# A fifth float16 tile for the attention weights, the position table made in place, and the weights' squares one row tile sooner

## The chip, the cores and the metric

The kernel runs on one core of one Trainium2 chip. Five engines work side by side, each with its own instruction queue executed in order: TensorE (PE, matrix products; its weight loads are listed as PEld), VectorE (DVE), ScalarE (ACT), GpSimd (POOL) and SyncE (SP), whose queue issues all of this kernel's DMA transfers. Tiles live in SBUF, with 128 partitions; matrix products land in PSUM banks. The metric is the time of one execution on the device in microseconds. Before the change it was measured in three runs: median 1084.36 us, 1083.74 to 1086.06.

## The reference

One layer on x of 1024 rows and 512 columns. After a layer norm, xn feeds an attention and a feed-forward network, and the output is x + attention * silu(ffn).

```python
q, k, v = xn @ Wq.T, xn @ Wk.T, xn @ Wv.T      # 32 query heads, 8 key/value heads, 128 wide
q, k = rmsnorm(q, q_norm_w), rmsnorm(k, k_norm_w)
scores = q @ k.T / sqrt(128)                   # four query heads share a key head
rel = pos[None, :] - pos[:, None]
bias = where(rel > 0, -1e30, slopes[head] * rel)
attn = softmax(scores + bias) @ v
s = attn @ Wo.T                                # to 512 columns
g = silu((silu(xn @ gate) * (xn @ up)) @ down) # dequantized int weights, 1792 wide
out = x + s * g
```

The slopes are a geometric series over the 32 heads: head i has `start * start**i` with `start = 2**(-0.25)`. Four heads on, the slope is half as large.

## The kernel before

**Precision.** Most operands are split into a high and a low part of float16 (or of a 32-bit format that TensorE takes in one pass), and a product is three matmuls: high by high, high by low, low by high (`mm3`, L106 to L110).

**Stages.** The feed-forward network comes first, up to about 216 us. Then twelve projections (L981), in the order kv, q, q four times over: each `kv` makes two key and two value heads, each `q` the four query heads of one group. The attention's steps begin between the row tiles of the last two projections and go on alone after them, to the end.

**A projection** goes through eight row tiles t of 128 rows. `tile(t)` (L543) is twelve matmuls into one PSUM bank of two tags with two buffers each, a copy to SBUF on ScalarE (L553) and, on ScalarE too, sums of squares (L555); in a `kv`, ScalarE also casts the value half (L567) and VectorE subtracts (L568). Between the row tiles the next projections are prepared (`prepare`, L641). For a projection k + 2, whose weights are loaded during t = 0 to 3, `squares` (L480) runs on ScalarE ahead of row tile 7: for a `q` four squares of 128 x 512 with their accumulated sums and a small cast to `sb`; for a `kv` two of these, the cast, and one square of 128 x 1024. In the next projection, ahead of row tile 1, `norms` (L492) multiplies `sb` by ones on TensorE (L496), and VectorE makes from it the scales by which the weights are split, a head for each row tile from t = 2. Each half of a projection's rows is normalised some steps later: POOL multiplies (L609), VectorE splits into halves (L621, L622), SP transposes (L627) and stores (L632, L634).

**The attention** has 128 units, in the order of 8 groups, 4 query blocks of 256 rows and 4 heads; the blocks of a group go by `ORDER` = 2, 3, 0, 1 (the first group 3, 2, 1, 0, the last 2, 3, 1, 0), so that blocks of up to 768, 1024, 256 and 512 keys follow each other. Each unit has two query tiles, and step n (L921) puts these on the queues:

- TensorE: `scores` of tile n into one of two double banks;
- ScalarE: `heads_hi` of a unit that is done; VectorE and ScalarE: `exponentials` of tile n - 1. VectorE adds the positions `trel[g]` to the scores into a float32 tile `pf` (five buffers) and takes the minimum (L814), which frees the bank; ScalarE takes the exponential with its sum (L815);
- ScalarE: `split_hi` of tile n - 3 writes the scaled high half into a `p16` tile (L825);
- VectorE: `split_lo` of tile n - 4 writes the low half into it (L834); SP transposes the tile by DMA into `pT` (L835);
- VectorE: `heads_lo` (L868) and the sums of the output projection;
- TensorE: `values` of tile n - 9 (`AV_LAG`), which takes half of the keys for both query tiles of a unit, and matmuls of the output projection.

The order on each queue is that of the program; nothing is reordered. A `p16` tile is 4096 bytes in each partition, and there are `P16_BUFS = 4` (L62): `split_hi` of a tile waits until the transpose of the fourth tile before it has landed.

**The positions.** L732 to L734 make once, on POOL, a float32 table `nrel` of 4096 bytes in each partition, an iota with 1e20 where a key lies after the query. `relative(g)` (L787) makes from it `trel[g]`, one of two buffers, times a factor `rc` of each partition and the slope of the group's last head (L790); VectorE multiplies by the head's ratio in L814. `relative(0)` is called ahead of projection 9, with the first loads of keys, values and queries (L982 to L986), the others in the third block of the group before.

Of the kernel before, what the change touches and what calls it, by code (L numbers as in the profile page):

```python
# [10 lines left out]
F32 = mybir.dt.float32  # L11
# [5 lines left out]
ALU = mybir.AluOpType  # L17
# [4 lines left out]
P = 128  # L22
S = 1024
# [3 lines left out]
NH = 4  # L27
# [3 lines left out]
NT = S // P  # L31
# [27 lines left out]
GATE_SUMS = [27, 28, 30, 31]  # L59
GATE_STEP = 2  # L60
PF_BUFS = 5
P16_BUFS = 4  # L62

_START = 2 ** (-(2 ** (-(math.log2(H) - 3))))
SLOPES = np.array([_START * _START**i for i in range(H)], dtype=np.float32)
# [5 lines left out]
def attention_gated_by_ffn_kernel(ctx, tc, x, gu_w, gu_z, gu_s, dn_w, dn_z, dn_s, wq, wkv, wo, qnw, knw, out):  # L71
    nc = tc.nc
    ve, se, ge, te, sp = nc.vector, nc.scalar, nc.gpsimd, nc.tensor, nc.sync
# [46 lines left out]
    rc = const.tile([P, 1], F32, name="rc")  # L120
# [334 lines left out]
    def finish_step():  # L455

        for f in finishing.pop(clock[0], ()):
            f()
        clock[0] += 1
# [181 lines left out]
    def prepare(k, t):  # L641

        if k < len(projections):
            p = projections[k]
            if t == -1:
                p.squares()
            elif t == 1:
                p.norms()
            elif t == 2:
                p.scale()  # L650
            elif t == 6:
                p.factors()
            if 2 <= t < 2 + p.n:
                p.split_head(t - 2)
            elif p.kind == "kv" and 4 <= t < 6:
                p.split_values(t - 4)
# [72 lines left out]
    vp16 = left.enter_context(tc.tile_pool(name="values", bufs=1))  # L729
    fq = ctx.enter_context(tc.tile_pool(name="finish", bufs=2, side="right"))  # L730
    ap1 = ctx.enter_context(tc.tile_pool(name="attn1", bufs=2, side="right"))
    nrel = ap1.tile([P, S], F32, name="nrel", bufs=1)  # L732
    ge.iota(nrel, pattern=[[-1, S]], base=S - P, channel_multiplier=1, allow_small_or_imprecise_dtypes=True)
    ge.affine_select(nrel, nrel, pattern=[[-1, S]], compare_op=ALU.is_ge, fill=1e20, base=S - P, channel_multiplier=1)  # L734

    def queue_half(p, half):

        last = p is projections[-1]

        def due(steps, i, f):  # L740
            t = half * HT + i
            c = TILES - early + BS * (NB * (1 + t // 2) + FINISH_BLOCK) + 4 * (t % 2) if last else clock[0] + i
            finishing.setdefault(c + steps, []).append(f)

        due(0, 0, lambda: p.inverse(half))
        if p.by_root:
            due(1, 0, lambda: p.newton(half, True))
        else:
            for i in range(3):
                due((i + 1) // 2, 0, lambda i=i: p.newton(half, i == 0))  # L750
        for i in range(HT):
            t = half * HT + i
            due(4, i, lambda t=t: p.halves(t))
            due(2, i, lambda t=t: p.normalize(t))
# [5 lines left out]
    trel, pT, oT, wor = {}, {}, {}, {}  # L760

    def load_keys(g):
        kT[g] = ap1.tile([P, NT, 2, P], F16, tag="kT", name=f"kT{g}")
        sp.dma_start(kT[g].rearrange("p t a k -> p t (a k)"), kd[g // 2][:, g % 2])

    def load_values(g):
        vT[g] = ap1.tile([P, NT, 2, HD], F16, tag="vT", name=f"vT{g}")
        sp.dma_start(vT[g].rearrange("p t a d -> p t (a d)"), vd[g])

    def load_queries(g, qb):  # L770
        qT[g, qb] = ap1.tile([P, NQT, 2, NH, P], F16, tag="qT", name=f"qT{g}_{qb}")
        sp.dma_start(
            qT[g, qb].rearrange("p t a g q -> p t (a g q)"), qd[g][qb * NQT : (qb + 1) * NQT].rearrange("t p c -> p t c")
        )
# [11 lines left out]

    def relative(g):  # L787

        trel[g] = ap1.tile([P, S], F32, tag="trel", name=f"trel{g}")
        ge.tensor_scalar(trel[g], nrel, rc, float(SLOPES[g * NH + NH - 1]), ALU.mult, ALU.mult)  # L790

    s_ps, pf, rows16, p16, av_ps, op_ps = {}, {}, {}, {}, {}, {}

# [24 lines left out]
    def split_hi(u, qt):  # L818
# [4 lines left out]
        nk = pf[u, qt].shape[1]  # L823
        p16[u, qt] = ap1.tile([P, NT, 2, P], F16, tag="p16", name=f"p16_{u}_{qt}", bufs=P16_BUFS)[:, :nk]
        se.activation(p16[u, qt][:, :, 0, :], pf[u, qt], AF.Copy, scale=scale[:, qt : qt + 1])  # L825
# [95 lines left out]
    def step(n):  # L921
        nonlocal last_ps
        if n < nn:
            u, qt = order[n]
            g, qb, hh = units[u]
            b = u // NH
            if qt == 0 and hh == 1 and b + 1 < nb:
                load_queries(*blocks[b + 1])
            if qt == 0 and hh == 3 and g + 1 < HKV:
                if b % NB == KEYS_BLOCK:  # L930
                    relative(g + 1)
                    load_keys(g + 1)
                elif b % NB == VALUES_BLOCK:
                    load_values(g + 1)
            scores(u, qt)
# [41 lines left out]
                act(w, r // 2)  # L977

    last_ps = None
    early = 0  # L980
    for k, p in enumerate(projections):  # L981
        if k == len(projections) - 3:  # L982
            load_keys(0)
            load_values(0)
            load_queries(*blocks[0])
            relative(0)  # L986
        for t in range(NT):
            prepare(k + 1, t)
            if t == NT - 1:
                prepare(k + 2, -1)  # L990
            if k + 2 < len(projections) and t < KT:
                projections[k + 2].load(t)
            if t == HT:
                p.undo()
            p.tile(t)
            finish_step()
            if t % HT == HT - 1:
                queue_half(p, t // HT)
            if k >= len(projections) - 2 and t % 2 == 0:
                step(early)  # L1000
                early += 1
# [46 lines left out]
```

## Time and profile before

| | |
|---|---|
| median of three runs | 1084.36 us |
| the profiled execution | 1086.72 us |
| its span, first to last instruction | 1084.9 us |
| TensorE busy | 1023.0 us, 94% |
| VectorE busy | 879.7 us, 81% |
| ScalarE busy | 796.2 us, 73% |
| POOL busy | 351.5 us, 32% |
| ScalarE's waits at L825 for a transpose to land | 73.6 us, 56 times |
| TensorE's waits at L108 for a transpose to land | 24.4 us, 18 times |
| mean granted TensorE clock | 0.99 |

The profile is one execution; its times are microseconds from the first instruction. A group of instructions is shown as line, engine, operation, tile written and tiles read, forms and count, then the busy time, the mean duration in ns, and the idle time of the engine just before, with what ended it. In the view of waits a line says who waited for whom, the sum, how often, and the longest. In the view by time a line has the start, the duration, the engine, line and operation, and in brackets the idle time of the engine before it. SPq is SP's queue, where the duration is that of the issue and not of the transfer. The ends of matmuls are modelled.

### The profile page before, as it was taken

To read this page: it belongs to the slowest core of one execution; us is meant where nothing else is said; L and a number is where in the kernel's file an instruction comes from. 1 tells how busy PE (TensorE), PEld (TensorE's weight loads), DVE (VectorE), ACT (ScalarE), POOL (GpSimd) and SP (SyncE) were. 2 spreads that over 40 slices of the span, in tenths; PEclk is the share of its full clock that TensorE was granted. 3 is DMA by queue.
4 is the path that set the end of the run, shared out by engine and by line. 5 is a ranking of instruction groups with operands and counts; after the bars stand their busy time and mean duration, and the time that the engine had idled before them with its cause. 6 is when DMAs were issued, how large, how long until landed. Compare 5 with 4: busy or idle time off the path is not lost.

```text
span 1084.9 us, 18415 instructions
## 1 busy us (share of the span) xinstructions
PE 1023.0 (94%) x5912; PEld 621.7 (57%) x5912; DVE 879.7 (81%) x1738; ACT 796.2 (73%) x2144; POOL 351.5 (32%) x343
## 2 busy tenths in 40 slices
PE   7899899999999999996999999999998999999996
PEld 5444378744444444444666666666665576676664
DVE  7888997438777896886898896998897978969974
ACT  5777633578687787786887796896886878868961
POOL 1588653115545556431105013023030030132222
PEclk8999999999999999999999999999999999999999
DMA  6133255237989999999999999998998999999994
GB/s 198 38 108 119 67 147 150 78 115 162 238 207 195 263 201 278 209 203 218 212 182 198 197 205 186 202 208 186 197 208 186 209 199 176 201 223 201 238 192 104
DMA packets 445888, 198.10 MB, mean 183 GB/s; under 512 B 394403, under 2 KB 403935, under 8 KB 445791
## 3 DMA queue, kind: packets, MB, share of 16 engines
q1 hardware_dynamic: 445790, 196.93, 82.7%
q8 instruction: 46, 0.75, 0.3%
q14 instruction: 52, 0.42, 0.1%
HBM read 71.03 MB, written 29.36 MB: 93 GB/s over the span
## 4 chain that ended last, share of the span: by engine, by line
PE 52%; DMA 15%; DVE 12%; ACT 11%; issue 7%; POOL 2%; SPq 0%; DVEq 0%; ACTq 0%; POOLq 0%
DMA pT<-p 13%; PE gu_ps L255 6%; PE s L108 3%; PE s L109 3%; PE s L110 3%; PE av L108 3%; PE ps_q L108 3%; PE ps_q L110 3%; PE ps_q L109 3%; PE op L108 3%; PE av L109 3%; ACT p L825 3%; PE av L110 3%; PE op L109 3%; PE op L110 3%
## 5 line engine op out<-in xcount | busy, mean ns | idle before, releaser
L834 DVE SCALAR_TENSOR_TENSOR p<-pf,row,p 128x1024 f16<-128x1024 f32 (+7 forms) x256 | 218.1, 852 | 76.9 <-ACT p L825 74.3
L825 ACT ACTIVATE p<-pf,row 128x1024 f16<-128x1024 f32 (+7 forms) x256 | 197.0, 770 | 76.9 <-DMA pT<-p 73.6
L815 ACT ACTIVATE pf<-pf,row 128x1024 f32<-128x1024 f32 (+7 forms) x256 | 197.2, 770 | 36.2 <-DVE row L814 34.2
L814 DVE CUSTOM_DVE_ANT_0 pf<-s,trel,cs 128x1024 f32<-128x1024 f32 (+7 forms) x256 | 207.2, 809 | 4.0 <-PE s L110 3.1
L785 POOL TENSOR_TENSOR wol<-wor,woh 128x512 fp32r<-128x512 f32 x32 | 58.5, 1828 | 433.7 <-ACT woh L784 433.7
L108 PE MATMUL av<-pT,vT 128*128 128x256 f16 (+1 forms) x640 | 171.7, 268 | 24.9 <-DMA pT<-p 24.4
L109 PE MATMUL av<-pT,vT 128*128 128x256 f16 (+1 forms) x640 | 169.0, 264 | 0.0
L110 PE MATMUL av<-pT,vT 128*128 128x256 f16 (+1 forms) x640 | 168.7, 264 | 0.0
L108 PE MATMUL s<-kT,qT 128*128 128x512 f16 (+3 forms) x384 | 125.5, 327 | 8.6 <-DVE row L814 8.4
L109 PE MATMUL s<-kT,qT 128*128 128x512 f16 (+3 forms) x384 | 125.6, 327 | 0.0
L110 PE MATMUL s<-kT,qT 128*128 128x512 f16 (+3 forms) x384 | 123.9, 327 | 0.0
L108 PEld LDWEIGHTS <-vT 128*128 128x128 f16 x640 | 62.6, 98 | 105.6 <-issue 80.5
L108 PE MATMUL op<-woh,oh 128*128 128x512 f32 x248 | 121.7, 491 | 0.0
L110 PE MATMUL op<-woh,ol 128*128 128x512 f32 x248 | 98.9, 399 | 0.0
L109 PE MATMUL op<-wol,oh 128*128 128x512 f32 x248 | 97.8, 394 | 0.0
L110 PE MATMUL ps_q<-wh_q,xtl 128*128 128x512 f16 x256 | 97.1, 379 | 0.0
L108 PE MATMUL ps_q<-wh_q,xth 128*128 128x512 f16 x256 | 97.1, 379 | 0.0
L109 PE MATMUL ps_q<-wl_q,xth 128*128 128x512 f16 x256 | 97.1, 379 | 0.0
L609 POOL TENSOR_TENSOR f_q<-f_q,inv_q 128x512 f32<-128x512 f32 x64 | 77.5, 1236 | 1.4
L862 ACT ACTIVATE oh<-av,rv 128x256 fp32r<-128x256 f32 x128 | 59.0, 461 | 23.6 <-PE av L110 23.1
L868 DVE SCALAR_TENSOR_TENSOR ol<-av,rv,oh 128x256 fp32r<-128x256 f32 x128 | 61.2, 478 | 14.2 <-ACT oh L862 14.1
L109 PEld LDWEIGHTS <-vT 128*128 128x128 f16 x640 | 63.7, 99 | 13.0 <-issue 3.7
(183 smaller groups left out, 2239.7 us busy)
## 6 DMA issues: line engine op xcount, KB each, us to landing
qd<-tr_q SPq DMA_DIRECT2D x64, 256.0 KB, 3.4
qT<-qd SPq DMA_DIRECT2D x32, 512.0 KB, 4.3
wq<-in_wq SPq DMA_DIRECT2D x32, 256.0 KB, 4.0
wor<-in_wo SPq DMA_DIRECT2D x32, 256.0 KB, 3.6
gui<-in_gu_w SPq DMA_DIRECT2D x13, 512.0 KB, 3.5
wkv<-in_wkv SPq DMA_DIRECT2D x16, 256.0 KB, 4.0
vd<-v SPq DMA_DIRECT2D x8, 512.0 KB, 3.9
kd<-tr_kv SPq DMA_DIRECT2D x32, 128.0 KB, 2.2
```

The costliest lines, as they stand in the source:

```text
L108: te.matmul(ps, lhsT=lh, rhs=rh, start=first, stop=False)
L109: te.matmul(ps, lhsT=lh, rhs=rl, start=False, stop=False)
L110: te.matmul(ps, lhsT=ll, rhs=rh, start=False, stop=last)
L255: te.matmul(banks[j][:, k, :], lhsT=w[:, j, ws], rhs=x[:, j, k * 512 : k * 512 + 512], start=x is xth, stop=x is xtl)
L609: ge.tensor_tensor(f, f, ib, ALU.mult)
L785: ge.tensor_tensor(wol[g, i], raw, woh[g, i].bitcast(F32), ALU.subtract)
L814: ve.tensor_tensor_reduce(p, ps, trel[g][:, S - w :], cs[:, hh : hh + 1], 3e38, ALU.add, ALU.min, least[:, c])
L815: se.activation(p, p, AF.Exp, bias=least[:, c], scale=-1.0, accum_out=total[:, c])
L825: se.activation(p16[u, qt][:, :, 0, :], pf[u, qt], AF.Copy, scale=scale[:, qt : qt + 1])
L834: ve.scalar_tensor_tensor(lo, p, scale, hi, ALU.mult, ALU.subtract)
L862: se.activation(oh, av_ps[u], AF.Copy, scale=rv[:, g : g + 1])
L868: ve.scalar_tensor_tensor(ol, av_ps.pop(u), rv[:, g : g + 1], oh.bitcast(F32), ALU.mult, ALU.subtract)
```

## The change

It has two parts.

**A fifth `p16` tile.** `P16_BUFS` becomes 5, which takes 4096 bytes in each partition; `nrel` goes, which gave as many. The iota and the select are now made in the buffer of `trel[0]` and scaled there, and every later `trel[g]` is its predecessor times one constant, the ratio of the two slopes (a half), without the factor `rc`. `relative(0)` is called ahead of all projections.

**The squares a row tile sooner.** `prepare(k + 2, -1)` stands ahead of row tile 6 (`NT - 2`) and no longer ahead of row tile 7. In ScalarE's queue the squares then come before the eviction of row tile 6.

```diff
-P16_BUFS = 4
+P16_BUFS = 5
...
-    nrel = ap1.tile([P, S], F32, name="nrel", bufs=1)
-    ge.iota(nrel, pattern=[[-1, S]], base=S - P, channel_multiplier=1, allow_small_or_imprecise_dtypes=True)
-    ge.affine_select(nrel, nrel, pattern=[[-1, S]], compare_op=ALU.is_ge, fill=1e20, base=S - P, channel_multiplier=1)
...
     def relative(g):
 
-        trel[g] = ap1.tile([P, S], F32, tag="trel", name=f"trel{g}")
-        ge.tensor_scalar(trel[g], nrel, rc, float(SLOPES[g * NH + NH - 1]), ALU.mult, ALU.mult)
+        rel = trel[g] = ap1.tile([P, S], F32, tag="trel", name=f"trel{g}")
+        if g == 0:
+            ge.iota(rel, pattern=[[-1, S]], base=S - P, channel_multiplier=1, allow_small_or_imprecise_dtypes=True)
+            ge.affine_select(rel, rel, pattern=[[-1, S]], compare_op=ALU.is_ge, fill=1e20, base=S - P, channel_multiplier=1)
+            ge.tensor_scalar(rel, rel, rc, float(SLOPES[NH - 1]), ALU.mult, ALU.mult)
+        else:
+            ge.tensor_scalar(rel, trel[g - 1], float(SLOPES[g * NH + NH - 1] / SLOPES[g * NH - 1]), None, ALU.mult)
...
     last_ps = None
+    relative(0)
     early = 0
     for k, p in enumerate(projections):
         if k == len(projections) - 3:
             load_keys(0)
             load_values(0)
             load_queries(*blocks[0])
-            relative(0)
         for t in range(NT):
             prepare(k + 1, t)
-            if t == NT - 1:
+            if t == NT - 2:
                 prepare(k + 2, -1)
```

## The prediction

> **What bounds the kernel now.** I read the page first, then TensorE's waits, then the queues in order of time at two places. The page has TensorE busy for 1023.0 of 1084.9 us and names one big idle time on ScalarE and one on VectorE:
>
> ```profile
> PE 1023.0 (94%) x5912; PEld 621.7 (57%) x5912; DVE 879.7 (81%) x1738; ACT 796.2 (73%) x2144; POOL 351.5 (32%) x343
> L834 DVE SCALAR_TENSOR_TENSOR p<-pf,row,p 128x1024 f16<-128x1024 f32 (+7 forms) x256 | 218.1, 852 | 76.9 <-ACT p L825 74.3
> L825 ACT ACTIVATE p<-pf,row 128x1024 f16<-128x1024 f32 (+7 forms) x256 | 197.0, 770 | 76.9 <-DMA pT<-p 73.6
> ```
>
> L825 writes the high half of a p16 tile and waits 73.6 us for the transpose that still reads the buffer: the wait that a fifth buffer loosens. But neither engine is the bound. What TensorE waits for after the FFN is short:
>
> ```profile
> PE av L108 <- DMA pT<-p: 24.4, 18, 2.8
> PE s L108 <- DVE row L814: 8.4, 13, 1.8
> PE n_ps L496 <- ACT sb_q L488: 4.3, 5, 1.4
> PE op_last L110 <- DVE ol L868: 2.1, 1, 2.1
> ```
>
> So the question is which of these ends sooner when ScalarE stops waiting. SP's queue, VectorE, ScalarE and TensorE in order of time, where a block of 896 to 1024 keys hands over to one of 128 to 256 (us from the start, us, engine and line):
>
> ```profile
> 652.54 8.11 SPq L835 DMA_TRANSPOSE pT<-p  x3
> 660.75 0.53 SPq L772 DMA_DIRECT2D qT<-qd  x1
> 661.39 8.76 SPq L835 DMA_TRANSPOSE pT<-p  x4
> ...
> 657.32 1.15 DVE L834 SCALAR_TENSOR_TENSOR p<-pf,row,p 128x896 f16<-128x896 f32 x1 [0.36 <-ACT p L825]
> 659.33 1.27 DVE L834 SCALAR_TENSOR_TENSOR p<-pf,row,p 128x1024 f16<-128x1024 f32 x1
> 668.85 0.35 DVE L834 SCALAR_TENSOR_TENSOR p<-pf,row,p 128x128 f16<-128x128 f32 x1 [3.79 <-ACT p L825]
> ...
> 668.42 0.40 ACT L825 ACTIVATE p<-pf,row 128x128 f16<-128x128 f32 x1 [4.53 <-DMA pT<-p]
> ...
> 670.01 0.27 PE L108 MATMUL av<-pT,vT 128*128 128x256 f16 x1 [2.52 <-DMA pT<-p]
> ```
>
> SP issues without a gap from 652.5 to 670.1. The two large tiles that TensorE misses at 670.01 were ready when VectorE ended (658.47 and 660.60); SP came to them at 661.39 and 664.47, 2.9 and 3.9 us late. ScalarE's 4.53 us wait lies beside this: the tile it holds up is ready at 669.20, SP gets to it at 670.88. I followed the other stalls of this kind back along SP's queue: all through 472 to 534 (five stalls) and at each hand-over from the largest block it was issuing, or held by a transfer not yet landed. Only before two (0.51 at 690.4, 1.32 at 1062.7) had it waited for L834, and there ScalarE had not waited for a buffer. These 24.4 us are the queue's and stay.
>
> **The change, part by part.** *Fifth p16 tile.* It lets ScalarE go one tile further; at 668.42 the next tile would then wait for the same landing. TensorE gains only where VectorE, held up behind L834, was late with L814 for a score bank (8.4 us). Before 500 us this is 3.6, of which 3.2 (at 486.5 and 490.4) have ScalarE busy with evictions and exponentials, not waiting. The other nine, 4.7 us: 0.47 (611.6), 0.88 (741.0), 0.34 (762.3) and 0.34 (837.2) are each followed within 19 us by an av stall of 0.27, 1.33, 1.00 and 1.67 that SP's queue sets; TensorE coming sooner waits longer there, so I count 0.20 of these 2.03. 0.94 (985.0) follows an L834 of 1.82 us instead of 0.75, no wait for p16. Left are 0.18, 0.41, 0.54, 0.63 (621.1, 903.0, 974.9, 977.1) and the 0.20: 1.96, taken as -2.0, between 0 and -8.4.
>
> *The end.* ScalarE waits 3.20 us at 1062.12 for a p16 buffer, VectorE 3.00 with it; ol, for which op_last waits 2.11, comes after three more L834. With five buffers the first L834 runs at about 1059.6; the second needs the landing at 1062.04 and L825 after it (0.5), so it starts at 1062.6, not 1063.45. The rest of VectorE's row moves up by 0.85, and TensorE's waits of 0.38 and 2.11 shrink by that together: -0.85, between 0 and -2.5. The gate loads beside it still set the 1.32 us at 1062.66.
>
> *Squares one row tile sooner.* For a q projection ScalarE issues four squares with their reads and a cast (300.76 to 304.02: 3.26 us), for kv two and one of 1024 columns; no DMA moves. They pass exactly one eviction, that of row tile 6: 1.03 us when the running projection is kv, 1.47 when it is q. Only so much sooner is sb ready, for ScalarE is behind there:
>
> ```profile
> 299.73 0.40 ACT L553 COPY f_kv<-ps_kv 128x256 f32<-128x256 f32 x1
> 300.76 0.69 ACT L485 ACTIVATE sq_q<-wq 128x512 bf16<-128x512 f32 x1
> ...
> 304.08 0.16 PE L496 MATMUL n_ps<-sb_q,ones_bf 128*128 128x4 bf16 x1 [1.31 <-ACT sb_q L488]
> ...
> 425.55 0.70 SPq L478 DMA_DIRECT2D wq<-in_wq  x1
> 430.89 0.63 ACT L485 ACTIVATE sq_q<-wq 128x512 bf16<-128x512 f32 x1 [0.25 <-DMA wq<-in_wq]
> ```
>
> The five waits at L496 (304.1, 346.6, 368.9, 411.4, 434.2) are 1.31, 0.40, 1.41, 0.41, 0.74. They lose 1.03, 0.40, 1.03, 0.41 and 0: the last squares wait for weights that land at 430.87, and ScalarE would now stand there from 429.46. Sum 2.87. What is late next is row tile 6's own eviction, by 3.3 us (4.6 in projection 9); its bank is used again 5.8 us later or more (6.1 there), so cover is left, 1.5 us at the least. If it were gone, TensorE would lose each further microsecond.
>
> How much of 2.87 arrives SP decides. Behind the late eviction stands VectorE too, when the running projection is kv: its v (L568) of row tile 6, then the halves of the q projection before, whose transposes SP issues in order. In projections 3 and 6 SP took that transpose 0.5 and 1.1 us after the halves (302.83, 303.35; 367.63, 368.75), and waited for the next (0.88 and 0.28 us of gap before 306.63 and 371.43). With halves some 2.8 us later, the first transpose comes 1.7 to 2.3 later and the queue is about 1.4 behind at 306 and at 371. From 371 on it never stands at VectorE's heels again: q and k wait 2.5 to 7.3 us for it up to 485, its 7.9 us of gaps from 385 to 488 are mostly waits for landings, and it sets TensorE's five stalls up to 534. What TensorE has gained by then it would wait longer for pT. At 371 the queue stands 1.43 ahead (the 1.03 and 0.40 before) less those 1.4. I take -0.5, between -4.3 and +1.5.
>
> *The table.* The iota (0.99) and the select (1.04) stay; their buffer is now trel's. The first scaling (1.12) moves from 411.40 to about 221.3 on POOL, which is idle from there until 234.76; rc is long computed. The seven later ones lose the factor rc and read the predecessor: 1.17 each today, no less than the select's 1.04, so 0 to -0.9 on an engine that is idle 68% of the span. The new reading of a live tile waits for nothing: VectorE only reads it too, and the buffer written was last read a group earlier. If that cover were gone, one scaling would be 1.2 us late for a block that needs it eight steps on. Cost 0.
>
> *Rule against row.* Three full transposes (1024, 896, 1024 keys) hold SP for 8.11 us, 2.70 a step, while TensorE takes 2.19 a step (av starts at 656.37, 658.56, 660.75): the queue falls behind. The Trainium skill, DMA: Bandwidth & Descriptors, section Latency and other measured facts, gives the DMA transpose an effective 261 GB/s in the worse case; these 1.51 MB would be an estimated 5.8 us, under TensorE's 6.6, the queue would have room, and the 24.4 us would be the buffers': a sum of some -28 in place of -3.35. The row decides.
>
> *Sum.* -2.0 - 0.85 - 0.5 + 0 = -3.35. The profiled execution took 1086.72 (span 1084.9, 1.8 around it) and would take 1083.4; it is 2.36 above the median of the three timed runs (1084.36), so the forecast is 1084.36 - 3.35 = **1081.0 us**.
>
> **Rivals.** *Nothing arrives.* The score waits come back as waits for pT at the next hand-over, and SP takes all of the squares' gain; the end and about 0.5 remain: 1084.36 - 1.35 = 1083. For it: 2.03 us of score waits already stand ahead of such stalls. Against: in every block of 640 to 768 keys SP waits for VectorE, so a gain made after a group's last stall (903.0, 974.9, 977.1) is passed on.
>
> *The squares arrive whole.* SP's gaps give way and attention starts 2.87 sooner: 1084.36 - 2.0 - 0.85 - 2.87 = 1078.6. For it: SP caught up at 306 and 371. Against: from 414 three loads of 0.5 MB for attention are added to its queue.
>
> *The buffers were on the path.* A tile ready sooner is issued sooner, and part of the 24.4 us goes too. For it: SP's own waits name L834 54 times, 52.9 us. Against: it waited so before two stalls alone. With half of the 24.4: 1081.0 - 12.2 = 1069.
>
> *Slower: VectorE behind the squares.* The delay above, at its full price. It decides where SP's lag behind the halves is under the 3.3 us that the cast comes later and SP sets the pace: 0.5 us in projection 3, 1.1 in 6, 4.3 in 9. Two places cost 2.8 at 1.4 each and 6.6 at 3.3 each, and the squares' gain goes: 1084.36 - 2.85 + 2.8 to 6.6 = 1084.3 to 1088.1, about 1087. Against: up to 486 TensorE waits for nothing but L496 and once for a score bank (0.52).
>
> **How the numbers follow.** About 0.2% (2.2 us) is what a measurement of this kernel can tell from no change. Forecast 0.38 (its own range 1078 to 1082.2), nothing arrives 0.30, squares whole 0.10, buffers 0.05, slower 0.17. Faster 0.38 + 0.10 + 0.05 = 0.53, within 0.30, slower 0.17. Low end 1075: squares 2.9, score waits 4.7, end 2.0, together 9.6. High end 1087: the slower rival's middle. Outside are the buffers' rival and the upper half of the slower one.
>
> **What would show it.** L825's wait for pT falls from 73.6 to some 50 to 60 and L834's with it; av's waits for pT stay within 20 to 28; L496's fall from 4.3 to about 1.5; score waits from 8.4 to 5 or 6; op_last's to about 1.3; the transposes before 306 and 371 come 1.4 to 2.3 us later against TensorE. POOL has one operation early and the rest unchanged. Wrong if av's waits fall below 15, if SP's transposes of 1024 keys take other times, or if ScalarE waits for wq at more places than projection 9.

## The result, and the profile after

The changed kernel took 1082.55 us (median of 14 runs, 1078.74 to 1087.19), the kernel before, on the same chips, 1084.10 (14 runs, 1079.36 to 1086.06). The ratio is 0.9989 with a 95% interval of 0.9974 to 1.0004: 1.2 us less, between 2.8 less and 0.4 more, so no difference is shown. The profiled execution took 1087.19 us, its span is 1085.4.

The page of the changed kernel, engines' totals and the two groups that write a `p16` tile (L825 is now L827, L834 is L836):

```profile
PE 1025.6 (94%) x5912; PEld 621.8 (57%) x5912; DVE 885.4 (82%) x1738; ACT 797.9 (74%) x2144; POOL 362.7 (33%) x343
L836 DVE SCALAR_TENSOR_TENSOR p<-pf,row,p 128x1024 f16<-128x1024 f32 (+7 forms) x256 | 216.4, 845 | 39.2 <-ACT p L827 36.3
L827 ACT ACTIVATE p<-pf,row 128x1024 f16<-128x1024 f32 (+7 forms) x256 | 196.9, 770 | 34.1 <-DMA pT<-p 30.1
```

ScalarE's wait for a transpose to land fell from 73.6 to 30.1 us, and VectorE's behind it from 74.3 to 36.3. The view of waits says what TensorE got of that (sum, times, longest), and what ScalarE waits for that it did not before:

```profile
PE av L108 <- DMA pT<-p: 25.4, 23, 2.7
PE s L108 <- DVE row L816: 3.8, 4, 1.8
ACT sq_kv L485 <- DMA wkv<-in_wkv: 3.4, 2, 2.2
PE n_ps L496 <- ACT sb_q L488: 2.9, 2, 2.0
ACT sq_q L485 <- DMA wq<-in_wq: 2.2, 1, 2.2
PE op_last L110 <- DVE ol L870: 1.7, 1, 1.7
PE n_ps L499 <- ACT sq_kv L490: 1.4, 2, 0.8
```

TensorE waits for `pT` as long as before (25.4 against 24.4), for score banks less than half as long (3.8 against 8.4). The waits at L496 fell from 4.3 to 2.9, but one of 1.4 at L499 is new, and smaller new ones are not shown: 0.6 at L496 for a `kv`, 0.8 and 0.6 for split weights. Above all ScalarE now stands 5.6 us, in projections 4, 7 and 9, before weights that have not landed.

The hand-over that the prediction showed, in order of time in the changed kernel:

```profile
655.96 8.18 SPq L837 DMA_TRANSPOSE pT<-p  x3
664.23 0.53 SPq L769 DMA_DIRECT2D qT<-qd  x1
664.87 9.17 SPq L837 DMA_TRANSPOSE pT<-p  x4
...
667.37 0.40 ACT L827 ACTIVATE p<-pf,row 128x128 f16<-128x128 f32 x1
671.87 0.51 ACT L827 ACTIVATE p<-pf,row 128x256 f16<-128x256 f32 x1 [3.46 <-DMA pT<-p]
...
673.64 0.27 PE L108 MATMUL av<-pT,vT 128*128 128x256 f16 x1 [2.58 <-DMA pT<-p]
```

It is the same picture. ScalarE gets one tile further (the 128-key tile at 667.37 no longer waits) and stands before the next one for 3.46 us; SP holds three large transposes for 8.18 us (8.11 before), and TensorE misses the same tiles for 2.58 us (2.52).

Where the gain went is in the projections. Around the end of projection 6, VectorE, SP, ScalarE and TensorE of the changed kernel:

```profile
369.81 0.42 DVE L568 TENSOR_TENSOR v<-ps_kv,v 128x256 f16<-128x256 f32 x1 [2.57 <-ACT v L567]
370.61 0.98 DVE L622 TENSOR_TENSOR q<-f_q,q 128x512 f16<-128x512 f32 x1
...
368.63 0.57 SPq L632 DMA_DIRECT2D qd<-tr_q  x1
371.62 1.24 SPq L627 DMA_TRANSPOSE tr_q<-q  x1
...
384.47 0.57 SPq L478 DMA_DIRECT2D wkv<-in_wkv  x1
...
388.51 0.63 ACT L485 ACTIVATE sq_kv<-wkv 128x512 bf16<-128x512 f32 x1 [2.19 <-DMA wkv<-in_wkv]
...
390.26 0.16 PE L496 MATMUL n_ps<-sb_kv,ones_bf 128*128 128x2 bf16 x1 [0.58 <-ACT sb_kv L488]
391.22 0.60 PE L499 MATMUL n_ps<-sq_kv,ones_bf 128*128 128x256 bf16 x4 [0.80 <-ACT sq_kv L490]
```

The same work in the kernel before, VectorE's halves, SP's transpose behind them, the last load and the first square:

```profile
366.94 0.69 DVE L622 TENSOR_TENSOR q<-f_q,q 128x512 f16<-128x512 f32 x1
...
368.75 1.28 SPq L627 DMA_TRANSPOSE tr_q<-q  x1
...
380.90 0.58 SPq L478 DMA_DIRECT2D wkv<-in_wkv  x1
...
386.13 0.66 ACT L485 ACTIVATE sq_kv<-wkv 128x512 bf16<-128x512 f32 x1
```

Read the changed kernel's lines downwards. The squares stand ahead of row tile 6's eviction, so VectorE's `v` (L568) waits 2.57 us for its cast, and the halves of the query tile behind it are done at 371.59 (367.63 before). SP stands idle for them from 369.20 to 371.62. The weight loads for the next `kv` are behind that transpose in SP's queue: the last is issued at 384.47 (380.90 before). So the squares that read these weights, moved a row tile sooner in the program, start at 388.51 and not at 386.13: later than before. TensorE's product waits for them.

### The profile page after: what moved, and what is told of

The parts are those of the page before. It is cut to its first block, busy times and chain, and to the rows that moved or that the text cites. A ratio compares the mean times of both kernels' runs of the same rounds, so it can differ in the third digit from the quotient of the medians.

```text
span 1085.4 us, 18417 instructions
## 1 busy us (share of the span) xinstructions
PE 1025.6 (94%) x5912; PEld 621.8 (57%) x5912; DVE 885.4 (82%) x1738; ACT 797.9 (74%) x2144; POOL 362.7 (33%) x343
## 4 chain that ended last, share of the span: by engine, by line
PE 57%; DVE 12%; ACT 11%; DMA 10%; issue 6%; POOL 2%; SPq 0%; DVEq 0%; ACTq 0%; POOLq 0%
DMA pT<-p 9%; PE gu_ps L255 6%; PE av L108 4%; PE s L108 4%; PE av L110 4%; PE av L109 4%; PE s L109 4%; PE s L110 4%; PE op L108 3%; PE op L110 3%; PE op L109 3%; ACT p L827 3%; PE ps_q L109 2%; PE ps_q L108 2%; PE ps_q L110 2%
## 5 line engine op out<-in xcount | busy, mean ns | idle before, releaser
L836 DVE SCALAR_TENSOR_TENSOR p<-pf,row,p 128x1024 f16<-128x1024 f32 (+7 forms) x256 | 216.4, 845 | 39.2 <-ACT p L827 36.3
L827 ACT ACTIVATE p<-pf,row 128x1024 f16<-128x1024 f32 (+7 forms) x256 | 196.9, 770 | 34.1 <-DMA pT<-p 30.1
L108 PE MATMUL av<-pT,vT 128*128 128x256 f16 (+1 forms) x640 | 171.8, 268 | 25.6 <-DMA pT<-p 25.4
```

The source lines that it names most:

```text
L108: te.matmul(ps, lhsT=lh, rhs=rh, start=first, stop=False)
L836: ve.scalar_tensor_tensor(lo, p, scale, hi, ALU.mult, ALU.subtract)
```

## The experiments

**1. The fifth tile alone.** The table goes with it; the squares stay.

```diff
-            if t == NT - 2:
+            if t == NT - 1:
                 prepare(k + 2, -1)
```

> The fifth p16 tile and the table in place, the squares left ahead of row tile 7. My theory (the buffers are off the path): TensorE's waits av <- DMA pT stay at 22 to 27 us (before 24.4), ScalarE's wait for pT falls to 30 to 35 us as in the full change, the score waits go from 8.4 to 4 to 6 us, and the time is 1081 to 1083, 1 to 3 us under before. Rival (the buffers are on the path): av's waits fall under 15 and the time under 1076. Rival (nothing arrives): what the score banks give is waited for at the next hand-over, av's waits grow by it, and the time is within 1 us of before.

Measured: 1078.05 us (12 runs) against 1082.88 (20 runs), ratio 0.9952 (0.9936 to 0.9967): 5.2 us less, between 3.6 and 6.9. The kernel with the fifth tile alone:

```profile
ACT p L827 <- DMA pT<-p: 29.3, 27, 3.3
PE av L108 <- DMA pT<-p: 26.9, 22, 2.9
PE s L108 <- DVE row L816: 4.1, 4, 1.8
```

TensorE's waits are as my theory had them, ScalarE's 29.3 us lie just under its 30 to 35. The rival that has the buffers on the path is out: TensorE's waits for `pT` rose by 2.5 us. So is *nothing arrives*. The time fell further than the 1 to 3 us expected. This half of the change by itself beats both kernels.

**2. The squares alone.**

```diff
-            if t == NT - 1:
+            if t == NT - 2:
                 prepare(k + 2, -1)
```

> Only the squares ahead of row tile 6; four p16 tiles and the old table. My theory (SP's queue gives the gain back): TensorE's waits for sb at L496 fall from 4.3 to 1.5 to 3 us, and the first step of attention begins no sooner than before, or later by up to 4 us; the time is within 1 us of before. Rival (slower): VectorE's row tile 6 stands behind the squares, SP runs behind the halves by 5 to 9 us after 371 instead of 2.5 to 7.3, and the time is 2 to 4 us over before. Rival (the squares arrive whole): attention starts 2.9 us sooner and the time is 2.9 under before.

Measured: 1087.68 us (9 runs), ratio 1.0051 (1.0031 to 1.0071): 5.5 us more, between 3.4 and 7.7. My theory fell, the slower rival holds, at or over the upper end of its 2 to 4 us. From the end of projection 0 to the first `split_hi` it took 227.6 us in place of 221.3. Where projection 10 begins, ScalarE, TensorE and VectorE of this kernel:

```profile
433.72 0.63 ACT L485 ACTIVATE sq_q<-wq 128x512 bf16<-128x512 f32 x1 [2.98 <-DMA wq<-in_wq]
...
436.98 0.16 PE L496 MATMUL n_ps<-sb_q,ones_bf 128*128 128x4 bf16 x1 [2.77 <-ACT sb_q L488]
...
438.02 0.42 DVE L568 TENSOR_TENSOR v<-ps_kv,v 128x256 f16<-128x256 f32 x1 [5.65 <-ACT v L567]
...
443.41 0.38 PE L108 MATMUL s<-kT,qT 128*128 128x512 f16 x1 [1.07 <-DVE am_q L501]
```

In projection 9 SP's queue holds the first loads for attention as well, and `wq` lands at 433.7, not at 430.9. ScalarE stands 2.98 us before it with row tile 6's eviction behind it, TensorE 2.77 for `sb`, VectorE 5.65 at L568. VectorE is then so late that it has not read the norms (L501) when the scores need that bank, 1.07. TensorE's waits account for an estimated 6.1 us of the longer stretch: 2.6 more at the starts of projections 5 and 8 and 2.0 more in projection 10, all behind squares that stood before weights; 1.4 for split weights that ScalarE makes behind the squares; the 1.07; 1.3 for eight more waits, each of which costs 0.16 beyond its length (worked out behind the experiments); less 2.3 gained at the other four of the five waits at L496.

**3. Half transposes.** Of each tile's key tiles only the first half is transposed, and the values' products read it twice; the attention's values are left incomplete.

```diff
         sp.dma_start_transpose(
-            pT[u][:, :nk, :, qt * P : qt * P + P].rearrange("p t a q -> p (t a) q"), h16.rearrange("p t a k -> p (t a k)")
+            pT[u][:, : (nk + 1) // 2, :, qt * P : qt * P + P].rearrange("p t a q -> p (t a) q"),
+            h16[:, : (nk + 1) // 2].rearrange("p t a k -> p (t a k)"),
         )
...
-                (pT[u][:, kt, 0, c0:], pT[u][:, kt, 1, c0:]),
+                (pT[u][:, kt % per, 0, c0:], pT[u][:, kt % per, 1, c0:]),
```

> The kernel before, with only the first half of each p16 tile's key tiles transposed (from 8 of 8 to 4 of 8 at 1024 keys); the values' products read that half twice, so the number of matmuls is the same and the attention's values are left incomplete. My theory (the 24.4 us of av's waits are SP's queue and its transfers): with half the bytes a step holds SP for 1.35 us instead of 2.70, under TensorE's 2.19, av's waits fall from 24.4 to under 6 us with four buffers still, ScalarE's wait for pT from 73.6 to under 20, and the time falls by 15 to 22 us to 1062 to 1069. Rival (the waits are VectorE's or ScalarE's pace, the queue only passes it on): av's waits stay over 15 and the time falls by less than 8.

Measured: 1051.50 us (4 runs), ratio 0.9713 (0.9687 to 0.9740): 31 us less, more than the 15 to 22 expected. Its waits, and SP's issue of the three transposes that took 8.11 us in the kernel before:

```profile
ACT p L825 <- DMA pT<-p: 13.9, 13, 3.0
PE s L108 <- DVE row L814: 5.6, 9, 1.8
PE av L108 <- DMA pT<-p: 1.5, 2, 0.8
...
639.47 4.89 SPq L835 DMA_TRANSPOSE pT<-p  x3
```

With four buffers still, the 24.4 us are down to 1.5. They belong to SP's queue and its transfers, as the prediction had it. The score waits fell by 2.8 besides, and the clock never fell in attention (last section). The waits make 25.7 of the 35.6 us by which the profile of before is longer; 22 fewer waits in attention at 0.16 and three fewer falls of the clock at 1.7 add an estimated 8.6, and 1.3 stay open. This run does not separate the time that SP is held from the time that the bytes travel.

**4. Half transposes with the squares moved.** Experiments 2 and 3 together.

> As the run with half transposes, with the squares ahead of row tile 6 as well; the same part of the attention is left out. Where SP's queue no longer sets TensorE's stalls in attention, what the squares gain in the projections has nothing left to wait for. My theory: 1 to 3 us under the run with half transposes alone. Rival (the squares cost as much in the projections themselves, by VectorE's later values and the wait for wq in projection 9): within 1 us of it or over it.

Measured: 1055.62 us (4 runs), ratio 0.9750 (0.9719 to 0.9781), 4 us over experiment 3. The two intervals overlap, but the runs of the two do not (1051.1 to 1051.9 and 1055.1 to 1058.8). My theory fell: even where SP's queue hardly delays attention, the squares cost about as much. What they cost is lost in the projections: from the end of projection 0 to the end of the last one the trace of 4 is 4.8 us longer than that of 3.

**5. The fifth tile in the last group alone.** From experiment 1, with one extra buffer that only tiles from `FIVE_FROM = 112` on take, the first unit of the last group.

```diff
-        p16[u, qt] = ap1.tile([P, NT, 2, P], F16, tag="p16", name=f"p16_{u}_{qt}", bufs=P16_BUFS)[:, :nk]
+        n = 2 * u + qt - 2 * FIVE_FROM
+        fifth = n >= 0 and n % P16_BUFS == 0
+        p16[u, qt] = ap1.tile(
+            [P, NT, 2, P], F16, tag="p16x" if fifth else "p16", name=f"p16_{u}_{qt}", bufs=1 if fifth else P16_BUFS - 1
+        )[:, :nk]
```

> Squares ahead of row tile 7, table in place, and the fifth p16 tile used in the last group of heads alone (the last 32 of 256 tiles, from about 990 us on); four before. The fifth tile in all groups was worth 0.48%. My theory from its trace: with the clock's dips left out TensorE lost 3.35 us less after 1020 us, and some 2.6 less between 540 and 1020; so the last group alone gives 2.5 to 4 us, TensorE's waits after 1020 are 2.5 us in sum instead of 5.9, and the score waits before it stay at 7 to 9. Rival (the forecast's term): the end is worth 0.85 and the time is within 1.5 us of before.

Measured: 1082.19 us (12 runs) against 1082.79 (23 runs), ratio 0.9998 (0.9982 to 1.0013). My theory, which I had read from one pair of traces, fell: the end is worth nothing that shows, and most of the gain lies in the groups before. What one pair of traces gives for a stretch of 80 us is not the change's.

**6. and 7. Weights loaded sooner, without and with the squares moved.** In 6 on the fifth tile alone, in 7 on the full change.

```diff
-            if k + 2 < len(projections) and t < KT:
-                projections[k + 2].load(t)
+            if k + 2 < len(projections) and t < KT // 2:
+                projections[k + 2].load(2 * t)
+                projections[k + 2].load(2 * t + 1)
```

> The fifth p16 tile and the table, squares ahead of row tile 7, and the four loads of a later projection's weights issued two each ahead of row tiles 0 and 1, in place of one each ahead of 0 to 3. My theory: weights land some 5 us sooner and transposes of q and k go behind them; ScalarE's wait for wq (1.2 us) goes, nothing else of TensorE's depends on it, so it is within 1.5 us of the run with the fifth tile alone (0.9952 of before). It is the reference for the next. Rival (the transposes pushed back delay attention): 2 us or more over it.

> The full change with the same early loads. My theory (the squares lose because, a row tile sooner, ScalarE stands waiting for weights that SP's queue has not brought, 5.6 us in three places, and the row tile's eviction behind them waits too): with the weights there, these waits fall under 1 us, TensorE's stalls between 230 and 490 us, 6.6 in the full change, fall under 4, and the time is within 1.5 us of the run before it in this list or up to 2.9 under it. Rival (VectorE's later halves and SP's later transposes are the cost, whenever the weights land): 3 to 5 us over it, as the full change is over the fifth tile alone.

Measured: 6 took 1076.41 us (6 runs), ratio 0.9944 (0.9926 to 0.9962), as expected within 1.5 us of experiment 1; 7 took 1079.80 (12 runs), ratio 0.9969 (0.9956 to 0.9982). In 7 ScalarE waits for no weights, and the squares still cost 2.7 us (7 over 6), near the rival's 3 to 5. So a good part of the price is there whenever the weights land. Without the early loads the squares cost 4.0 (the full change over experiment 1, 0.9989 to 0.9952); that the difference of 1.3 is the weights' is not shown, for the intervals are wider than that. ScalarE's largest sum of waits in the projections of 7, the eviction of a query row tile for an `f` buffer that VectorE has still to split, points to where:

```profile
ACT f_q L553 <- DVE q L622: 13.7, 6, 2.5
```

It is 9.4 us in 6. ScalarE delays VectorE, and VectorE, through the three `f` buffers, ScalarE. TensorE pays at two places above all: 2.03 us for `sb` at 410.93 (0.40 in 6) and 1.79 for the norms' bank at 441.00 (none in 6). That this loop leads to them is read from one pair of traces and was not tested by itself.

**8. Three tiles.** `P16_BUFS = 3` in the kernel before.

> The kernel before with three p16 tiles in place of four. My theory (the buffers reach TensorE through score banks alone): ScalarE's wait for pT rises from 73.6 to 120 to 160 us, the score waits from 8.4 to 15 to 25, TensorE's waits av <- DMA pT stay within 20 to 32, and the time rises by 5 to 15 us. Rival (the buffers set how far the transposes can run ahead): av's waits rise by 15 us or more and the time by over 20.

Measured: 1109.87 us (4 runs), ratio 1.0255 (1.0231 to 1.0279): 27.6 us more.

```profile
ACT p L825 <- DMA pT<-p: 109.5, 83, 4.7
PE s L108 <- DVE row L814: 43.9, 50, 2.7
PE av L108 <- DMA pT<-p: 3.0, 4, 1.4
```

The size is almost twice the upper end of what I expected, the way is the one of my theory; the rival had the size, but its way, longer waits for `pT`, is not what happened. Too few buffers hold up ScalarE, then VectorE, and reach TensorE as score banks that are not free (8.4 to 43.9). The waits for `pT` do not grow but nearly vanish, for a TensorE that is late finds its transposes landed.

**9. The squares cut in two.** On experiment 6: half of the heads ahead of row tile 6, the rest and the cast ahead of row tile 7.

```diff
-            if t == NT - 1:
-                prepare(k + 2, -1)
+            if t >= NT - 2:
+                prepare(k + 2, -2 if t == NT - 2 else -3)
...
+            elif t == -2:
+                p.squares(range(p.n // 2))
+            elif t == -3:
+                p.squares(range(p.n // 2, p.n))
```

> The fifth p16 tile, the early loads, and the squares cut in two: those of the first half of the heads ahead of row tile 6, the rest with the cast ahead of row tile 7, so that row tile 6's eviction stands behind 1.6 us of squares and not behind 3.3. Its reference is the run with the fifth tile and the early loads (0.9944 of before; five waits at L496, 3.9 us). My theory (the price is the length that stands ahead of one eviction, because VectorE's v and halves follow it): sb is ready up to 1.5 us sooner, the waits at L496 fall under 1.5 us, VectorE's delay is half as long, and the time is 0 to 3 us under the reference. Rival (any square ahead of that eviction is paid for): half of what the whole move costs there, 1.3 us over the reference.

Measured: 1075.80 us (6 runs), ratio 0.9933 (0.9917 to 0.9948); its interval and that of 6 overlap. The waits for `sb` are 3.5 us in place of 3.9, not under 1.5, and 2.3 us for the norms' bank are new. Not settled between the two. It is level with 6 as the fastest kernel here that leaves nothing out.

**10. Half transposes with the fifth tile.** Experiments 1 and 3 together.

> Half of each tile's key tiles transposed (the attention's values are left incomplete, as in the other run with half transposes), with the fifth p16 tile and the table in place, squares ahead of row tile 7. My theory (the fifth tile acts only through landings that come late): with half transposes ScalarE waits 13.9 us for pT with four tiles, so a fifth has little left to loosen: under 2 us below the run with half transposes and four tiles (0.9713 of before), where with whole transposes it gives 5.2. Rival (the gain is in the table, or in VectorE's and POOL's work): 3 to 5 us below it.

Measured: 1048.85 us (4 runs), ratio 0.9685 (0.9670 to 0.9701), 3.0 us under experiment 3 with overlapping intervals. Of these the traces give 1.05 to TensorE's waits from 440 us on (8.81 in 3, 7.76 here) and 1.6 to those at L496 (5.4 and 3.8), where `wq` landed sooner for projection 11. The first is under my 2 us; the time alone does not decide, but the table, which the rival names, is out by experiment 11.

**11. The table alone.** From experiment 1, `P16_BUFS = 4`.

> The kernel before with the table made in place alone: four p16 tiles, squares ahead of row tile 7, the 4096 bytes of the old table unused. It asks what of the 5.2 us of the fifth tile and the table together is the table's. The forecast's term: 0, the time within 1 us of before, ScalarE's wait for pT at 70 to 77, score waits at 7 to 9. Rival (the scalings without the factor of each partition, or the first one moved out of projection 9, give part of the 5.2): 1.5 to 3 us under before.

Measured: 1083.08 us (12 runs) against 1082.71 (23 runs), ratio 1.0000 (0.9981 to 1.0020). ScalarE waits 72.2 us for `pT`, score waits are 7.4. The table costs and gives nothing that shows, within some 2 us either way; the 5.2 us are the fifth tile's.

**12. The squares moved only beside a q projection.** On the kernel before.

```diff
-            if t == NT - 1:
+            if t == NT - (1 if k % 3 == 0 else 2):
                 prepare(k + 2, -1)
```

> The kernel before, with the squares ahead of row tile 6 only while a q projection runs (1, 2, 4, 5, 7, 8, 10) and ahead of row tile 7 as before while a kv runs (0, 3, 6, 9). Theory A (the price is VectorE's v standing behind the squares, which only a kv projection has): within 1 us of before. Theory B (the price is ScalarE standing for weights that SP's queue brings late, which the run with the squares alone showed for wkv in projections 4 and 7): TensorE's waits at the start of projections 5 and 8, 1.3 us each with the squares alone, are there, and the time is 1.5 to 4 us over before, against 5.4 for the whole move. Between the two the loss is split over both kinds.

Measured: 1083.86 us (12 runs), ratio 0.9998 (0.9979 to 1.0016). Theory A holds. TensorE's two waits of 0.40 and 0.41 beside q projections are gone, and in projection 7 the squares for the next `kv` start without a wait at 382.82, on weights of which the last landed at 382.74. ScalarE's standing before `wkv`, 4.2 us in experiment 2 in just such q projections, is 0.7 here. So it is not a cause of its own: it is what the kv projection ahead has done to SP's queue. The squares moved beside kv projections alone were not run; that these carry the price follows from experiment 2 less this one.

## Why the prediction was right and wrong

The forecast was 1081.0 us, the time 1082.55 is inside the range and nearest to the rival *nothing arrives* (1083). But that rival's reason is not the reason. One half of the change gave more than forecast, the other took nearly all of it back. That the sum fell into the range is luck: fifth tile and end were forecast at -2.85 and gave -5.2, the squares at -0.5 and cost 4.0 to 5.5.

*The 24.4 us are the queue's and stay.* Right: 25.4 after, 26.9 with the fifth tile alone, 1.5 with half transposes (experiment 3). The rival *the buffers were on the path* (1069) is out. So is the Trainium skill's rate as the measure of this queue (DMA: Bandwidth & Descriptors, section Latency and other measured facts, 261 GB/s, which made an estimated 5.8 us of three transposes): they hold SP for 8.18 us after the change too.

*Fifth p16 tile, -2.0, and the end, -0.85.* The term was undersized: 5.2 us by the times of experiment 1. ScalarE's wait was forecast at 50 to 60 us and is 30.1, so VectorE comes to the score banks sooner than I allowed. Four profiles with four tiles (before, experiments 2, 11, 12) have score waits of 8.4, 7.1, 7.4 and 6.5, together 43 waits; five with five tiles (after, 1, 6, 7, 9) have 3.8, 4.1, 4.1, 4.3 and 2.6, 18 waits. That is 3.57 us and 7.2 waits less for a profile. The two at 491.35 and 495.29 that I left standing do stand (0.93 and 1.82); together they are 2.75, not the 3.2 that I wrote, and the two smaller ones before 500 us, 0.52 and 0.37, which I put at nothing without a reason, are 0.24 and gone. Each wait that is gone takes another 0.16 us with it, by which the matmul ahead of the wait lasts longer (128x512 float16: 0.38 us ahead of a wait, against 0.22 from one start to the next in an unbroken row): 1.15. I counted 0.20 of 2.03 us because av stalls follow; the waits for `pT` rose by 1.43 only (24.25 to 25.68 in the mean of the same profiles). Together -3.57 - 1.15 + 1.43 = -3.3. The end is not part of it: `op_last` waits 0.3 to 2.1 us with four tiles from profile to profile and 1.2 to 1.7 with five, and experiment 5 gave nothing. Between 3.3 and 5.2 (3.6 to 6.9) some 2 us stay open. From the end of the last projection on the four profiles take 599.9 us in the mean and the five 594.8, so the gain lies in attention; the falls of the clock that go with stalls, below, cost an estimated 6.5 and 5.5 of these, so they may be a part of what is open, but the profiles are too few to show that.

*Squares a row tile sooner, -0.5 between -4.3 and +1.5.* This step failed, and in sign: +5.5 alone, +4.0 in the full change. The first half of its working was half right: of the five waits at L496, 1.31, 0.40, 1.41, 0.41 and 0.74, three fell to 0.14, 0 and 0, one to 0.83. The fifth grew to 2.04, where I had written a loss of 0. What I called late next, row tile 6's eviction, had its bank's cover and was not the trouble. What stood behind it in VectorE's queue was, and I let it end as a lag of 1.4 us on SP. I did not follow it one step on: SP's queue also carries the weights of the projection after, and the squares wait for these. The line under which I wanted to be wrong, that ScalarE waits for `wq` at more places than projection 9, came true in kind: at two more places it waits for `wkv` (3.4 us). The transpose ahead of 371 came 2.87 us later by the time in the trace and 3.0 against TensorE's matmuls beside it, not 1.4 to 2.3.

*Slower: VectorE behind the squares.* This rival named the first part of the mechanism, VectorE and SP, and its place: the kv projections (experiment 12). It did not have the weights that come late behind it. It priced the squares at 2.8 to 6.6; alone they cost 5.5. It missed the time of the whole because it had the fifth tile and the end at 2.85 and not at 5.2.

*The table, 0.* Right (experiment 11).

## What to carry to other kernels

Putting work sooner in an in-order queue makes all that is behind it later: follow the delayed instruction through every queue, the DMA queue too, until it comes back to the operands of the work that was moved. Try the parts of a change apart, for +5.5 and -5.2 together looked like nothing. Take a buffer count's worth from what the engine that waits holds up, not from the length of its wait: from four to five tiles its wait fell by 44 us and the time by 5 (experiment 1), from three to four by 36 and 28.

## What the runs showed of the hardware

TensorE's granted clock fell to 0.50 for 3.41 us at a time, once for twice that (6.83 us, experiment 8). From 215 us to 8 us before the end each fall came after a stretch of 3.41 us in which TensorE had been idle more than half of the time. Windows of 3.41 us of the changed kernel, in pairs: length, busy time (count) of PE, PEld, DVE, ACT and POOL, then the granted clock, DMA share and GB/s:

```profile
435.49:438.90 3.41, 1.37 (x8) 0.61 (x7) 0.26 (x1) 3.31 (x15) 1.79 (x4) 1.00 1.20 248
438.90:442.31 3.41, 3.41 (x9) 1.18 (x8) 3.27 (x9) 1.45 (x8) 0.00 (x0) 0.50 1.09 266
...
821.19:824.60 3.41, 1.49 (x15) 1.14 (x15) 1.72 (x6) 2.22 (x9) 0.00 (x0) 1.00 0.75 141
824.60:828.01 3.41, 3.41 (x13) 2.00 (x12) 0.94 (x2) 0.41 (x2) 0.00 (x0) 0.50 0.76 161
```

Laid out back to back from such a fall, all 25 windows of the fourteen profiles with TensorE busy for a share of 0.41 or less were followed by one at half clock, 5 of the 24 with a share of 0.42 to 0.49, and one of some 3400 with more: the first half of the 6.83 us, itself at half clock, with 0.64. The grid starts elsewhere in each run, so the same stall halves the clock in one run and not in the next: one of 2.28 us at 667.5 does in experiment 1, one of 2.25 at 672.4 does not in experiment 2. The profile of before has three such falls between 215 us and the last stalls, that of the changed kernel five (one at 438.9, behind the 2.04 us wait that the squares made), that of experiment 1 one. A fall costs TensorE an estimated 1.7 us, half of 3.41, and the time of one kernel's runs goes with the clock: of 20 runs of the kernel before, four with a mean clock under 0.990 took 1084.9 to 1085.7 us, six with 0.994 or more 1078.2 to 1084.3. Thus a stall can cost more than its length, which my sums left out.

The Trainium skill (TensorE: Matmul & The Clock Gate, section What's actually happening) has the window of about 3.4 us, free-running, and the half clock after an idle one; these runs agree on the length and on the grid that starts elsewhere in each run. They add that a window need not be idle: none of the 25 above was (0.13 to 0.41 busy).
